# Depthwise taps on TensorE for two images, an offsets' chain with fewer steps, and normalisation over 128 partitions

## The chip, the cores and the metric

The kernel runs on one core of a Trainium2 chip. Its time is the device time of that core in microseconds (us). Five engines work side by side, each through its own instructions in order: TensorE (PE; its weight loads are listed as PEld), VectorE (DVE), ScalarE (ACT), GpSimd (POOL) and SyncE (SP). Transfers are issued by SP, ACT and POOL and run on 16 DMA engines. TensorE's clock is granted in shares of full speed, and the profile shows the share.

## The reference

Two layers over 32 images of 96 channels, 56 x 56, float32. Layer 0 is an inverted bottleneck with squeeze and excitation; layer 1 an attention by spectrum and space, a deformable convolution mixed by a gate with an ordinary one, and a normalisation over the whole batch.

```python
# layer 0
h = silu(bn(conv1x1(x, fake_quant(w1)), g1, b1, m1, v1))            # 96 -> 576
h = silu(bn(depthwise3x3(h, fake_quant(w2)), g2, b2, m2, v2))
s = sigmoid(se_w2 @ silu(se_w1 @ mean(h) + se_b1) + se_b2)
x = x + bn(conv1x1(h * s, fake_quant(w3)), g3, b3, m3, v3)          # 576 -> 96
# layer 1
mag = abs(rfft2(x));  ca = channel_attention(mag);  sa = spatial_attention(x, mag)
y = x * ca * sa
aux = concat([y, coord, freq_e], 1)                                 # 96 + 4 + 1 channels
offset = conv3x3(aux, off_w, off_b)                                 # 18 = 9 taps x 2
gate = sigmoid(conv1x1(relu(conv3x3(aux, dg1_w, dg1_b)), dg2_w, dg2_b))
y_base = conv3x3(y, base_w, base_b)
y_def = einsum(bilinear_samples(y, position + offset), def_w) + def_b
z = (1 - gate) * y_base + gate * y_def
zn = (z - mean(z)) / sqrt(var(z) + 1e-5) * bn_g + bn_b              # over batch and image
return relu(zn + x)
```

## The kernel before, in words

**Layer 0, first part** (`hidden`, with `expand`). An image's 576 hidden channels go in nine units: four chunks of 128 channels by two halves of 28 rows, and one unit that holds both halves of the last 64 channels. `expand` makes a unit's input: a matmul (L163) of seven or eight rows of x (the tile xt, one for each half image, two buffers) and a SiLU on ACT (L167) into one of two padded tiles hp. DVE then does the nine taps of the depthwise convolution on 128 x 1568 elements: a multiply (L224) and eight multiply-adds (L226) into acch. While it does, the next unit is expanded. `finish` applies the second SiLU on ACT (L208), sums for the squeeze, and stores the unit to DRAM (h2d). xt is loaded at the head of `hidden` (L198).

**Layer 0, second part, and the attention** (`attend`). It starts with `squeeze` (L249 to L261), then projects eight row blocks: h2d is loaded again as hq (L274, eight buffers, five for a block), multiplied (L290), the residual is added on POOL (L409) and the sum stored as x1d. Then come two spectral transforms (`dft_mag`) with a chain of small steps between them, whose results are the channel gate ca, the spatial gate sa, and the row fq. The loop multiplies x1d by both into the padded tile yp, eight rows at a time (`refill`), which holds 101 channels: 96 of y, four of coordinates, one of frequency.

**A band** is eight rows of the output, seven to an image, 224 in all. `offsets` makes the sampling weights of one band, two bands ahead. One convolution (`joint_conv`, L548) gives the hidden layer of the gate, the 18 offsets, and 32 of the 96 outputs of the base convolution; a second one (L577) the other 64. DVE adds the offsets' bias (L595) and takes their largest magnitude (L609); POOL adds each position in its 4 x 4 block (L602); the sums go to DRAM (od, L605, issued on POOL) and come back spread over 112 partitions, one copy for each of eight places and fourteen tiles (ht, L614, on SP); ACT makes of them the hat function max(0, 1 - |p - i|) (L617, L618); four transfers issued on POOL (hd, L622) write it to DRAM, from where it is loaded in the layout of the weights for columns and rows (wc and wr, L633 and L634, on SP), and DVE multiplies them (L640). Sampling is then a matmul of blocks of y with these weights (L669), copied out by ACT (L673, L680) and reduced by the deformable convolution (L688). `combine` mixes with the gate, and z goes to DRAM (zd).

**What sets the order.** The parts are generators that give up control at each `yield`. The main loop walks over the bands; at each of the 17 slots of a band it takes a step of `offsets` and, by a due time, steps of two streams: the attention of the next image and the hidden layer of the one after. SP's transfers stay in the order in which the program states them; on the other engines a scheduler may move instructions. Before the main loop, image 0's hidden layer runs alone; then its attention runs, with one step of image 1's hidden layer for each of its steps; then yp is filled, and the offsets of bands 0 and 1 are made.

**The end** (`normalise`). The statistics of z give a scale and a shift for each channel. For each image z and x1d are loaded on 96 partitions (SP and ACT), multiplied and added on DVE (L1220), passed through a Relu on ACT (L1221) and stored (SP, L1222), with three buffers of each. A slower block for offsets that reach further than two pixels stands before it, under a condition; it doesn't run with these inputs.

Of the kernel before, what the change touches and what calls it, by code (L numbers as in the profile page):

```python
# [7 lines left out]
FP = mybir.dt.float32  # L8
# [18 lines left out]
CA = C + 5  # L27
NOFF, NTAP = 18, 9
PD = 2
# [37 lines left out]
HB = HH * W  # L67

# [119 lines left out]
def hidden(tc, p, x, h2d, pooled, defer):  # L188
# [4 lines left out]
    xts = []  # L193

    def rows_of(half):
        xt = p["xt"].tile([C, (HH + 1) * W], FP, name="xt")
        r0 = half * (HH - 1)
        nc.sync.dma_start(xt, x[:, r0 : r0 + HH + 1].rearrange("c h w -> c (h w)"))  # L198
        xts.append(xt)

    rows_of(0)
    rows_of(1)
# [10 lines left out]
    for u, (ch, half) in enumerate(UNITS):  # L213
        h1 = p["h1"]
        more = expand(nc, p, xts, UNITS[u + 1]) if u + 1 < len(UNITS) else iter(())
        acc = p["acch"].tile([128, HH, W], FP, name="acch")
        for n, k in enumerate((4, 0, 1, 2, 3, 5, 6, 7, 8)):
            dy, dx = divmod(k, 3)

            lo, hi = int(half == 0 and dy == 0), HH - int(half == 1 and dy == 2)  # L220
            win = h1[:, dy + lo : dy + hi, dx : dx + W]
            wk = w["w2"][:, ch, k : k + 1]
            if n == 0:
                nc.vector.tensor_scalar(acc, win, wk, None, ALU.mult)  # L224
            else:
                nc.vector.scalar_tensor_tensor(acc[:, lo:hi], win, wk, acc[:, lo:hi], ALU.mult, ALU.add)  # L226
# [163 lines left out]
def attend(tc, p, b, x, h2d, pooled, x1, given=False):  # L390
# [7 lines left out]
    if not given:  # L398
        yield from squeeze(nc, p, pooled)
        rows = [project_loads(nc, p, x, h2d, q) for q in range(2)]  # L400
# [161 lines left out]
def joint_conv(nc, p, yp, j):  # L562
# [4 lines left out]
    conv3(nc, pa[:, :BW], w["joint"], yp, CA, j)  # L567
# [6 lines left out]
    for k in range(NTAP):  # L574
# [3 lines left out]
                         yp[:C, r0 : r0 + RB, dx + PD - 1 : dx + PD - 1 + W], start=(k < 2), stop=(k > NTAP - 3))  # L578
    nc.scalar.activation(yb[:BC], pb[:BC, :BW], AF.Identity, bias=w["cv"]("base_b")[:BC])
# [4 lines left out]
def offsets(nc, p, yp, j, top, hids, ybs, hds):  # L584
# [8 lines left out]
    off = p["off"].tile([NOFF, NTX, 2, TP], FP, name="off")  # L593
    for s in range(2):
        nc.vector.tensor_scalar(off[:, :, s].rearrange("o t (r c) -> o t r c", r=TS),  # L595
                                pa[:, s * BW // 2 : (s + 1) * BW // 2].rearrange("o (r t c) -> o t r c", r=TS, t=NTX),
                                w["offc"], None, ALU.add)
    yield
    yield
    next(joint)  # L600
    at = p["off"].tile([NOFF, NTX, 2, TP], FP, name="at")
    nc.gpsimd.tensor_tensor(at.rearrange("o t s p -> o (t s) p"), off.rearrange("o t s p -> o (t s) p"),  # L602
                            w["place"].unsqueeze(1).to_broadcast([NOFF, 2 * NTX, TP]), ALU.add)
    od = p["dp"].tile([NTX, 2, NOFF, TP], FP, name="od")
    nc.gpsimd.dma_start(od.rearrange("t s o p -> o (t s) p"), at.rearrange("o t s p -> o (t s) p"))  # L605
    yield
    yield
    next(joint, None)
    nc.vector.tensor_reduce(top, off.rearrange("o t s p -> o (t s p)"), AX.X, ALU.max, apply_absolute_value=True)  # L609
    yield  # L610
    yield
    ht = p["ht"].tile([NTX * SB, 4, KP], FP, name="ht")
    src = od.rearrange("t s o p -> t (s o p)").unsqueeze(1).to_broadcast([NTX, SB, 4 * KP])
# [6 lines left out]
    hd = p["dp"].tile([SB, 4, NTX, KP], FP, name="hd")  # L620
    for x in range(4):
        nc.gpsimd.dma_start(hd[:, x].rearrange("i t n -> t i n"), ht[:, x])  # L622
# [3 lines left out]
def weights_load(nc, p, hd, h):  # L626

    src = hd.rearrange("i n t k -> i n (t k)")[:, :, h * NTH * KP : (h + 1) * NTH * KP]
    wc = p["wc"].tile([2 * NS, NTH * KP], FP, name="wc")
    wr = p["wr"].tile([2 * NS, NTH * KP], FP, name="wr")  # L630
    for s in range(2):
        ps = slice(s * NS, (s + 1) * NS)
        nc.sync.dma_start(wc[ps], src[:, 2 * s].unsqueeze(0).to_broadcast([SB, SB, NTH * KP]))  # L633
        nc.sync.dma_start(wr[ps], src[:, 2 * s + 1].unsqueeze(1).to_broadcast([SB, SB, NTH * KP]))  # L634
# [86 lines left out]
def constants(tc, ctx, a, p, gather=False):  # L721
# [34 lines left out]
    load("offc")  # L756
    load("place")
# [91 lines left out]
def padded(nc, p, a, images):  # L849

    cp = p["cp"]
    yps = [cp.tile([CA, HY, WY], FP, name=f"yp{i}") for i in range(images)]
    for t in yps:
        nc.gpsimd.memset(t, 0.0)
        nc.sync.dma_start(t[C : C + 4, PD : PD + H, PD : PD + W], a["coord"])
    p["s4"] = [cp.tile([H, 3, WP], FP, name=f"s4_{i}") for i in range(2)]
# [11 lines left out]
def layers(tc, a, dp, x1d, zd, stats, far):  # L868
# [8 lines left out]
    with ExitStack() as ctx:  # L877
# [12 lines left out]
        def first(b):  # L890
# [5 lines left out]
            return hidden(tc, p, a["x"][b], h2d, pooled, lambda end: later.append((slot + 3, end)))  # L896
# [15 lines left out]
        count = lambda it: sum(1 for _ in it)  # L912
        n_first = count(first(0))
        flush()
        ahead = first(1)
        n_second = 0
        for _ in second(0):
            n_second += 1
            next(ahead, None)
        for _ in ahead:  # L920
            pass
        flush()
# [61 lines left out]
        for r in range(RB, H + 1, RB):  # L984
            refill(0, r)
            flush()
# [6 lines left out]
        for n in range(2):  # L993
            for _ in find(n):
                pass
        n_loads = 0
# [64 lines left out]
        nc.vector.tensor_scalar(far, every, float(REACH), None, ALU.is_gt)  # L1061
# [136 lines left out]
def normalise(tc, a, x1s, zds, stats, out):  # L1198

    nc = tc.nc  # L1200
    with tc.tile_pool(name="nc", bufs=1) as cp, tc.tile_pool(name="np", bufs=3) as tp:
# [12 lines left out]
        inv, sh = bn_affine(nc, cp, col("bn_g"), col("bn_b"), mv[:, 0:1], mv[:, 1:2], "z")  # L1214
        for b in range(B):
            zt = tp.tile([C, HW], FP, name="zt")
            nc.sync.dma_start(zt, zds[b])  # L1217
            xt = tp.tile([C, HW], FP, name="xt")
            nc.scalar.dma_start(xt, x1s[b])  # L1219
# [168 lines left out]
```

## Time and profile before

| | us |
|---|---|
| median of 3 runs | 10260.73 |
| lowest, highest | 10227.61, 10273.77 |
| the profiled execution | 10321.4 |
| its span, from the first to the last instruction | 10319.6 |

How to read the lines that follow below. The busy line of the page gives for each engine busy time, its share of the span, and the instructions. The span is cut in 40 slices with a digit each for busy tenths; PEclk is the granted clock, in tenths. In a table by windows a row is a stretch of time with its length, then busy time and number of instructions of PE, PEld, DVE, ACT and POOL, then the mean granted clock, the mean busy share of the 16 DMA engines, and GB/s moved. A line of waits names who sat idle and at which line, whom it waited for, us in total, how often, and the longest. A group of instructions gives its line, engine, operation, tiles and shape, how often, then total busy us and mean ns.

Durations that the prediction uses, from the groups by shape:

| line, engine, what | mean us |
|---|---|
| L224 DVE, first tap, 128x1568 | 1.03 |
| L226 DVE, further taps, 128x1568 | 1.84 (median of all) |
| L714 DVE, 96x448 with PSUM | 0.679 |
| L715 DVE, 96x448 | 0.936 |
| L602 POOL, positions added, 18x448 | 2.01 |
| L622 POOL, one of four hd issues | 0.574 |
| L1220 DVE and L1221 ACT, 96x3136 | 3.48 and 2.91 |
| L465 ACT, 112x48 | 0.24 |

### The profile page before, as it was taken

To read this page: it belongs to the slowest core of one execution; us is meant where nothing else is said; L and a number is where in the kernel's file an instruction comes from. 1 tells how busy PE (TensorE), PEld (TensorE's weight loads), DVE (VectorE), ACT (ScalarE), POOL (GpSimd) and SP (SyncE) were. 2 spreads that over 40 slices of the span, in tenths; PEclk is the share of its full clock that TensorE was granted. 3 is DMA by queue.
4 is the path that set the end of the run, shared out by engine and by line. 5 is a ranking of instruction groups with operands and counts; after the bars stand their busy time and mean duration, and the time that the engine had idled before them with its cause. 6 is when DMAs were issued, how large, how long until landed. Compare 5 with 4: busy or idle time off the path is not lost. (4 is left out here: it accounts for less than half of the span.)

```text
span 10319.6 us, 123181 instructions
## 1 busy us (share of the span) xinstructions
PE 8859.1 (86%) x43334; PEld 5021.5 (49%) x43334; DVE 7420.8 (72%) x6882; ACT 5342.5 (52%) x10183; POOL 3623.7 (35%) x3759
## 2 busy tenths in 40 slices
PE   2689999999999999999999999999999999999930
PEld 1355555555555555555555555555555555455520
DVE  8677777777777777787777777777777777775322
ACT  1355555555555555555555555555555555554432
POOL 0133433434333344333333333343343343333200
PEclk7789999999999999999999999999999999999865
DMA  1345555554555555455555544555555455555379
GB/s 61 98 135 145 147 146 152 145 137 134 140 144 146 153 150 142 130 143 142 144 142 156 148 137 134 141 144 145 155 148 136 132 140 149 140 150 139 99 210 281
DMA packets 1007994, 1485.64 MB, mean 144 GB/s; under 512 B 619949, under 2 KB 769149, under 8 KB 998154
## 3 DMA queue, kind: packets, MB, share of 16 engines
q1 hardware_dynamic: 873656, 985.19, 36.8%
q0 software_dynamic: 84960, 220.52, 8.5%
q10 hardware_dynamic: 48754, 271.96, 7.2%
q8 instruction: 349, 5.72, 0.3%
q14 instruction: 275, 2.25, 0.1%
HBM read 1064.23 MB, written 412.65 MB: 143 GB/s over the span
## 5 line engine op out<-in xcount | busy, mean ns | idle before, releaser
L226 DVE SCALAR_TENSOR_TENSOR acch<-hp,w,acch 128x1568 f32<-128x1568 f32 (+1 forms) x2304 | 4380.6, 1904 | 33.2
L548 PE MATMUL mm<-yp,c_jointW 101*128 101x448 f32 x4032 | 1688.6, 573 | 11.7 <-DMA yp<-fqd 9.1
L651 POOL COPY ybl<-yp 96x448 f32<-96x448 f32 x896 | 1171.5, 1334 | 1231.0 <-PE mm L655 1230.7
L688 PE MATMUL pd<-v,c_def 128*96 128x224 f32 (+1 forms) x6272 | 1404.2, 373 | 77.1 <-ACT v L680 55.6
L163 PE MATMUL mm<-xt,w 96*128 96x392 f32 (+3 forms) x2688 | 1148.3, 566 | 212.3 <-DMA xt<-in_x 106.5
L669 PE MATMUL mm<-wc,yt 64*96 64x144 f32 x12544 | 1181.4, 302 | 107.8 <-ACT hp L167 57.1
L688 PEld LDWEIGHTS pd<-v,c_def 128*96 128x96 f32 (+1 forms) x6272 | 1033.5, 171 | 366.4 <-ACT v L680 86.4
L548 PEld LDWEIGHTS mm<-yp,c_jointW 101*128 101x128 f32 x4032 | 798.3, 200 | 832.5 <-issue 789.8
L640 DVE TENSOR_TENSOR wc<-wc,wr 128x1008 f32<-128x1008 f32 x448 | 565.8, 1263 | 886.5 <-DMA wr<-hd 771.7
L602 POOL TENSOR_TENSOR at<-off,c_place 18x448 f32<-18x448 f32 x224 | 448.5, 2002 | 1894.6 <-DVE off L595 1894.2
L669 PEld LDWEIGHTS mm<-wc,yt 64*96 64x96 f32 x12544 | 892.4, 163 | 446.4 <-issue 248.6
L290 PE MATMUL mm<-hq,w3s 128*96 128x392 f32 (+1 forms) x2560 | 996.1, 528 | 91.7 <-DMA hq<-h2d 85.0
L673 ACT COPY v<-mm 96x288 f32<-96x288 f32 (+1 forms) x2688 | 999.3, 440 | 100.8 <-PE mm L669 67.6
L167 ACT ACTIVATE hp<-mm,sh,inv 128x392 f32<-128x392 f32 (+2 forms) x1216 | 811.4, 670 | 417.6 <-DVE acch L226 207.5
L208 ACT ACTIVATE acch<-acch,sh,inv 128x1568 f32<-128x1568 f32 x288 | 487.1, 1691 | 987.2 <-DVE acch L226 941.5
L577 PE MATMUL mm<-yp,c_base0W 96*64 96x448 f32 x4032 | 988.9, 590 | 0.0
L622 POOL DMA_DIRECT2D hd<-ht x896 | 509.5, 574 | 785.6 <-ACT ht L618 683.9
L680 ACT COPY v<-v 32x448 f32<-32x448 f32 x1344 | 755.2, 562 | 29.1
L364 PE MATMUL mm<-s,c_GV 112*112 112x464 f32 x1536 | 690.9, 593 | 43.4 <-ACT v L673 36.1
L163 PEld LDWEIGHTS mm<-xt,w 96*128 96x128 f32 (+1 forms) x2688 | 382.8, 189 | 627.9 <-issue 368.4
L290 PEld LDWEIGHTS mm<-hq,w3s 128*96 128x96 f32 (+1 forms) x2560 | 394.4, 169 | 600.0 <-issue 521.3
L577 PEld LDWEIGHTS mm<-yp,c_base0W 96*64 96x64 f32 x4032 | 315.8, 145 | 595.6 <-issue 531.5
(188 smaller groups left out, 9423.3 us busy)
## 6 DMA issues: line engine op xcount, KB each, us to landing
h2d<-acch ACTq DMA_DIRECT2D x288, 784.0 KB
wc<-hd SPq DMA_DIRECT2D x896, 252.0 KB
wr<-hd SPq DMA_DIRECT2D x896, 252.0 KB
hq<-h2d SPq DMA_DIRECT2D x1024, 196.0 KB
x<-x1d SPq DMA_DIRECT2D x768, 98.0 KB
ht<-od SPq DMA_DIRECT2D x224, 252.0 KB
hd<-ht POOLq DMA_DIRECT2D x896, 63.0 KB, 5.4
xt<-in_x SPq DMA_DIRECT2D x64, 609.0 KB
```

Of the source, the lines that this page charges most:

```text
L163: nc.tensor.matmul(pt[p0 : p0 + w1.shape[1], : rows * W], w1, xts[hf][:, r0 * W : (r0 + rows) * W], start=True, stop=True)
L167: nc.scalar.activation(h1[lo:hi, row0 : row0 + rows, 1 : 1 + W], pt[lo:hi, : rows * W].rearrange("p (h w) -> p h w", h=rows), AF.Silu, bia ...
L226: nc.vector.scalar_tensor_tensor(acc[:, lo:hi], win, wk, acc[:, lo:hi], ALU.mult, ALU.add)
L290: nc.tensor.matmul(pt[:C, :EW], w3s[ps, ch], hq[ps], start=(i == 0), stop=(i == NCH - 1))
L364: nc.tensor.matmul(pt[: 2 * W, :n].rearrange("p (q u) -> p q u", q=NPB), w["GV"][:, g], m, start=(k == 0), stop=(k == 1))
L548: nc.tensor.matmul(view, weights[:, k], yp[:channels, r0 : r0 + RB, dx + PD - 1 : dx + PD - 1 + W], start=(k == 0), stop=(k == NTAP - 1))
L577: nc.tensor.matmul(pb[k % 2 * BC : (k % 2 + 1) * BC, :BW].rearrange("p (h w) -> p h w", h=RB), w["base"][:, k], yp[:C, r0 : r0 + RB, dx + ...
L651: nc.gpsimd.tensor_copy(yb[:, :, s], blocks)
L669: nc.tensor.matmul(pt[k][:C, (t - lo) * KP : (t - lo + 1) * KP], yt[ps, t], s[ps, t * KP : (t + 1) * KP], start=True, stop=True)
L673: nc.scalar.copy(v[:C, :, lo:hi, k].rearrange("c k t p -> c t k p"), pt[k][:C, : (hi - lo) * KP].rearrange("c (t k p) -> c t k p", t=hi - ...
L680: nc.scalar.copy(v[C:, 1 + 2 * i : 3 + 2 * i], v[i * QC : (i + 1) * QC, KA:])
L688: nc.tensor.matmul(out.rearrange("c q (t x) -> c t q x", x=TS), p["w"]["def"][ks, k], v[ks, k].rearrange("c t s (r x) -> c t (s r) x", r=T ...
```

## The change

Four parts.

1. **Depthwise taps by TensorE for images 0 and 1.** Three of the nine taps (3, 1 and 5) become matmuls with diagonal weights. `diagonals` builds the fifteen 128 x 128 diagonals on ACT, in the memory of one of the buffers v that the main loop uses later. Per unit twelve matmuls go to four PSUM banks; the first tap on DVE becomes four multiply-adds that read them, and five taps follow. Before the main loop the diagonals are dropped, and later images use nine taps on DVE.
2. **The order around images 0 and 1.** Image 1's hidden layer takes 0.45 steps (`SPREAD`) for each step of image 0's attention, of the filling of yp, and of the first two bands' offsets. In all images the xt halves of the next image are loaded during the hidden layer of the one before, at its units 5 and 8, and the first hq load stands ahead of the squeeze.
3. **The offsets' chain.** Position and bias come out of the joint convolution: yp gets three more channels (column, row, one), so that DVE only copies the offsets out of PSUM, and POOL's addition is gone. ht has the place as its outer index and the tile as its inner one, and one transfer issued on ACT writes hd where four on POOL did. A step is put between the second base convolution and the ACT instruction that copies it out; ht's load comes two steps later. The test for offsets that reach too far looks at place and offset together.
4. **Normalisation over 128 partitions.** Each image is taken as 128 rows of 2352 elements, three pieces of 784, each of one channel. Scale and shift are brought into that layout through DRAM. Loads are all on SP, stores on ACT, with four buffers.

```diff
+def diagonals(nc, p):
+    v = p["vp"].tile([128, NTAP, NTH, 2, TP], FP, name="v")
+    v = v.rearrange("p k t s n -> p (k t s n)")[:, : NCH * len(TPE) * 128].rearrange("p (c k m) -> p c k m", c=NCH, m=128)
+    for ch in range(NCH):
+        for i, k in enumerate(TPE):
+            nc.scalar.mul(v[:, ch, i], p["w"]["ident"], p["w0"]["w2"][:, ch, k : k + 1])
+    return v
...
-    rows_of(0)
-    rows_of(1)
+    xts = p.pop("xts", None) or [rows_of(x, 0), rows_of(x, 1)]
...
+        if xn is not None and u in (5, 8):
+            p.setdefault("xts", []).append(rows_of(xn, int(u == 8)))
...
+        if diag is not None:
+            for r0 in range(0, HH, ER):
+                pt = bank(p)[:, :EW].rearrange("p (h w) -> p h w", h=ER)
+                for i, k in enumerate(TPE):
+                    dy, dx = divmod(k, 3)
+                    lo, hi = rows_of_tap(dy)
+                    lo, hi = max(r0, lo), min(r0 + ER, hi)
+                    nc.tensor.matmul(pt[:, lo - r0 : hi - r0], diag[:, ch, i], h1[:, dy + lo : dy + hi, dx : dx + W],
+                                     start=(i == 0), stop=(i == len(TPE) - 1))
+                parts.append((slice(r0, r0 + ER), pt))
...
+                for rs, pt in parts:
+                    nc.vector.scalar_tensor_tensor(acc[:, rs], win[:, rs], wk, pt, ALU.mult, ALU.add)
+                if not parts:
+                    nc.vector.tensor_scalar(acc, win, wk, None, ALU.mult)
...
+        rows = [project_loads(nc, p, x, h2d, 0)]
         yield from squeeze(nc, p, pooled)
-        rows = [project_loads(nc, p, x, h2d, q) for q in range(2)]
+        rows.append(project_loads(nc, p, x, h2d, 1))
...
-    conv3(nc, pa[:, :BW], w["joint"], yp, CA, j)
+    conv3(nc, pa[:, :BW], w["joint"], yp, CJ, j)
...
+    yield
     nc.scalar.activation(yb[:BC], pb[:BC, :BW], AF.Identity, bias=w["cv"]("base_b")[:BC])
...
-        nc.vector.tensor_scalar(off[:, :, s].rearrange("o t (r c) -> o t r c", r=TS),
-                                pa[:, s * BW // 2 : (s + 1) * BW // 2].rearrange("o (r t c) -> o t r c", r=TS, t=NTX),
-                                w["offc"], None, ALU.add)
-    yield
-    yield
-    next(joint)
-    at = p["off"].tile([NOFF, NTX, 2, TP], FP, name="at")
-    nc.gpsimd.tensor_tensor(at.rearrange("o t s p -> o (t s) p"), off.rearrange("o t s p -> o (t s) p"),
-                            w["place"].unsqueeze(1).to_broadcast([NOFF, 2 * NTX, TP]), ALU.add)
+        nc.vector.tensor_copy(at[:, :, s].rearrange("o t (r c) -> o t r c", r=TS),
+                              pa[:, s * BW // 2 : (s + 1) * BW // 2].rearrange("o (r t c) -> o t r c", r=TS, t=NTX))
+    yield
...
-    hd = p["dp"].tile([SB, 4, NTX, KP], FP, name="hd")
-    for x in range(4):
-        nc.gpsimd.dma_start(hd[:, x].rearrange("i t n -> t i n"), ht[:, x])
+    hd = p["dp"].tile([4, SB, NTX, KP], FP, name="hd")
+    nc.scalar.dma_start(hd.rearrange("x i t n -> (i t) x n"), ht)
...
-            zt = tp.tile([C, HW], FP, name="zt")
-            nc.sync.dma_start(zt, zds[b])
-            xt = tp.tile([C, HW], FP, name="xt")
-            nc.scalar.dma_start(xt, x1s[b])
-            nc.vector.scalar_tensor_tensor(zt, zt, inv, xt, ALU.mult, ALU.add)
-            nc.scalar.activation(zt, zt, AF.Relu, bias=sh)
-            nc.sync.dma_start(out[b].rearrange("c h w -> c (h w)"), zt)
+            zt = tp.tile([128, NQ * QW], FP, name="zt")
+            nc.sync.dma_start(zt, flat(zds[b]))
+            xt = tp.tile([128, NQ * QW], FP, name="xt")
+            nc.sync.dma_start(xt, flat(x1s[b]))
+            for i in range(NQ):
+                part = slice(i * QW, (i + 1) * QW)
+                nc.vector.scalar_tensor_tensor(zt[:, part], zt[:, part], qv[:, 0, i : i + 1], xt[:, part], ALU.mult,
+                                               ALU.add)
+                nc.scalar.activation(zt[:, part], zt[:, part], AF.Relu, bias=qv[:, 1, i : i + 1])
+            nc.scalar.dma_start(flat(out[b].rearrange("c h w -> c (h w)")), zt)
```

## The prediction

> **What bounds the kernel now.** I read the page first, then busy time by stage, then the waits of TensorE and of ScalarE, then short windows around one image's start.
>
> ```profile
> PE 8859.1 (86%) x43334; PEld 5021.5 (49%) x43334; DVE 7420.8 (72%) x6882; ACT 5342.5 (52%) x10183; POOL 3623.7 (35%) x3759
> ...
> PEclk7789999999999999999999999999999999999865
> DMA  1345555554555555455555544555555455555379
> ```
>
> The shares are averages over stages with different limits. Cut at the first depthwise tap (96 us), at the end of image 0's hidden layer (243), at its last attention step (446), at the first sampled tile (492) and at the last band (9901), and with two short windows behind:
>
> ```profile
> 96.00:243.00 147.00, 45.81 (x97) 18.09 (x95) 143.73 (x89) 37.16 (x56) 0.00 (x0) 0.55 0.18 63
> 243.00:446.00 203.00, 116.48 (x382) 63.58 (x383) 159.02 (x122) 69.07 (x117) 30.97 (x35) 0.70 0.31 95
> 446.00:492.00 46.00, 35.72 (x127) 17.39 (x127) 11.66 (x21) 10.08 (x17) 15.67 (x22) 0.83 0.43 105
> 492.00:9901.00 9409.00, 8654.15 (x42717) 4918.41 (x42716) 6937.34 (x6360) 5125.36 (x9951) 3568.12 (x3685) 0.93 0.52 142
> 9901.00:10320.00 419.00, 0.00 (x0) 0.00 (x0) 113.12 (x43) 94.52 (x34) 0.00 (x0) 0.50 0.97 277
> 220.00:240.00 20.00, 0.24 (x2) 0.16 (x2) 19.89 (x13) 4.10 (x6) 0.00 (x0) 0.50 0.10 40
> 9912.00:9936.00 24.00, 0.00 (x0) 0.00 (x0) 4.10 (x2) 2.91 (x1) 0.00 (x0) 0.50 1.01 227
> ```
>
> Columns: PE, PEld, DVE, ACT, POOL busy, granted clock, DMA share, GB/s. 96 to 243 is DVE's (143.7 of 147): nine units of nine taps, with TensorE two thirds idle and at 0.55 of its clock. 492 to 9901 is TensorE's (92%): 224 bands of 42.0 us. 9901 to the end is DMA's (0.97), at 277 GB/s.
>
> TensorE is in order, so each of its 755 idle us in the long stage is on the path. Who ended them, and where ScalarE, which TensorE waits for, was itself held up:
>
> ```profile
> PE mm L290 <- DMA hq<-h2d: 85.0, 35, 4.3
> PE acc L249 <- ACT acch L208: 84.7, 28, 3.6
> ...
> PE mm L163 <- DMA xt<-in_x: 72.9, 29, 6.6
> PE mm L669 <- ACT hp L167: 57.1, 42, 4.4
> PE pd L688 <- ACT v L680: 55.6, 56, 6.1
> ```
> ```profile
> ACT yb L579 <- PE mm L577: 482.8, 214, 6.6
> ...
> ACT ht L617 <- DMA ht<-od: 325.0, 107, 8.1
> ```
> ```profile
> 3736.00:3742.00 6.00, 4.20 (x21) 2.05 (x19) 5.34 (x6) 1.78 (x2) 0.51 (x1) 1.00 1.03 197
> 3742.00:3748.00 6.00, 1.75 (x4) 0.62 (x4) 2.62 (x4) 2.22 (x6) 1.63 (x2) 0.54 0.79 243
> 3748.00:3754.00 6.00, 6.00 (x19) 1.89 (x18) 0.00 (x0) 0.73 (x1) 0.35 (x1) 0.61 0.43 118
> ```
>
> The last fence is the wait for xt at one image's start (4.20 us, after 1.86 us for the squeeze, L249): the granted clock falls to 0.54 and 0.61 for two windows, and comes back. A wait costs its own length and slow matmuls behind it.
>
> **The tail: normalisation.** An image moves 3 x 96 x 3136 x 4 B = 3.61 MB. From the first zt load (9905.9) to the end (10319.6) are 413.7 us, 12.9 an image. DVE and ACT need 3.48 + 2.91 us of it and are hidden. After, they are three pieces of 784 of 3136 columns each: by width 2.6 and 2.2 us, hidden as well. What decides is the rate of transfers over 128 partitions, 9,408 B each. The trace of before has no such load. Bounds: loads of 96 partitions alone run at 227 GB/s with all engines busy (9912 to 9936); the store of 128 partitions (h2d, 0.8 MB) alone moves 40 GB/s at a share of 0.10 (220 to 240), so 400 GB/s at a full share. The new transfers are nearest to the second; I take 385 for loads and stores mixed: 9.4 us an image, 301 for 32. In front comes a new chain: two copies (0.15 us each, as L105), then a DMA to DRAM and one back, each about 2.1 us as sad<-sa, the second issued on SP with all later loads behind it: 5 us. Behind the last load remain DVE, ACT and a store, 9. Sum 315, gain 99; bounds +5 (rate as now) to -111 (400 GB/s: 289 + 14).
>
> [...]
>
> **The first 492 us.** Per unit DVE loses a multiply of 1.03 us (L224) and eight taps of 1.84 (L226), 15.75 us; it gains four 128x392 operations with PSUM and five taps. The nearest row for the first is L714 (96x448 from PSUM, 0.68 us), by width 0.60 (bounds 0.46, at L226's rate, to 0.94, L715's mean): 4 x 0.60 + 5 x 1.84 = 11.6. TensorE gains twelve 392-column matmuls, two records each. Ten records of L290 took 3.62 us at clock 1.00: 0.36 a record, 8.7 us a unit, with expand's four 11.5; at half clock 23. So the two engines come out even, and the clock decides. Since TensorE would be busy almost throughout, as in 256 to 272 where its clock was 1.00, I take the full clock. Unit 0 gains nothing (its taps wait for the first bank, which waits for all of hp), eight units 4.15 each: -33 for image 0. At half clock +60. The 15 diagonals on ACT (15 x 0.3 us; L465, 112x48, took 0.24) lie in its idle time before 89.7, where it waits for the first xt; uncovered 4.5.
>
> Image 1: attention of image 0 has 61 steps, the rows' fill 7, two offset chains 26; at 0.45 that pulls 42 steps, and the layer has 40, so nothing is left over. Six units fall in 243 to 446 and three in 446 to 492. In the first stretch DVE falls from 159 by 9 x 15.75 - 6 x 11.6 = 72 us, but the attention's own hops between engines bind: without the other image its second transform alone took 36 us (410 to 446). In the second stretch TensorE gets 3 x 11.5 on top of 35.7 of 46. I take -23 and +23, so 0; bounds -60 to +30.
>
> **The long stage.** (a) xt of the next image is loaded at units 5 and 8 of the one before, into buffers whose last readers are done: -72.9, and of the clock lost behind it. At 3742 that was 0.46 x 1.75 + 0.39 x 6.00 = 3.1 us; for 29 waits 90, of which I take half, since the squeeze's wait just ahead stays: -45. On SP the two loads stand behind no new wait, about a unit ahead. (b) POOL loses the addition (2.0 us x 224) and three of the four hd issues move away with the fourth to ACT (896 x 0.574). POOL is 38% busy: nothing by itself. But od leaves POOL one step and an addition earlier, while ht's use comes two steps later; with 17 steps a band of 42 us a step is 2.5 us, so the slack of ht grows by some 9 us, over the 8.1 of ACT's longest wait for it. And the extra step ahead of L579 lets ACT do other work while TensorE makes the base convolution. That removes most of 808 us in which ACT stood blocked. TensorE's own waits for ACT (hp, v, yt, sq, without the squeeze) sum to 208 us; bounds 0 to -208, and I take a third, -70, since its stalls also come from ACT's length. (c) ACT gains 224 DMA issues of 0.33 us, 74 us of its 4284 idle. DVE's copies for additions are the same count and size: 0. (d) hq's first load ahead of the squeeze: the wait I looked at (3818) lies at a late row block, held by the eight hq buffers, which stay: 0, bound -85. Sum -188, bounds 0 and -450.
>
> **Sum.** -99 - 33 + 0 - 188 = -320. The profiled execution took 10321.4 (span 10319.6), 0.6% over the median of 10260.73. Made against its own time it is 10001; carried to the median, 9941. I say **9940**.
>
> **Rivals.**
> - Long stage unchanged but for a part of xt: TensorE's stalls for ACT come from the waits for TensorE in a ring (L569 <- L548, 789 us, stays), and the clock still falls behind L249, L383, L499. Then -99 - 33 - 50: 10080. For: the clock is 0.93 on average, and most of the large waits of the list are not touched.
> - The tail's rate is bound behind the partitions, by memory: the share is already 0.97 and a mixed window of 12.9 us averages 280 GB/s. Gain at most 20 there: 10020. Against: 227 and 400 GB/s at full share, by kind.
> - Slower: the hat weights land late. hd now leaves at step 13 instead of 11, 5 us later, less 1.7 for three POOL issues; wc and wr follow it on SP, and DVE already waits 771.7 us for wr in 234 waits, with taps and products queued behind. If TensorE stalls at L669 for it by 1 us in each of 448 halves, +448: 10390. It decides against the gain from 320 / 448 = 0.71 us a half. Against: hd is read half a band (21 us) later, and TensorE waited for wc only once (9.5 us).
> - The diagonals at half clock: DVE waits for TensorE in both images, +60 + 33 and as much in 243 to 492: some 10090.
>
> **Chances.** Forecast, 9830 to 10010: 0.56. Long stage unchanged: 0.18. Tail bound elsewhere: 0.09. Diagonals slow: 0.06. More than forecast (ACT's waits go with their clock): 0.05. Slower: 0.06, a third of which ends within 0.5%. Range 9800 to 10120. A measurement of this kernel can tell 0.5% (51 us) from nothing; by these cases faster 0.93, same 0.03, slower 0.04.
>
> **What would show it.** The stage without TensorE falls from 419 to about 320 at 370 to 400 GB/s. The hidden layer of image 0 takes about 110 us with TensorE's clock near 1; if it stays at 0.55 the step on the clock was wrong. In the long stage the wait for xt is gone, ht's and L579's waits on ACT are under 150 together, and the granted clock is over 0.94; if ACT's waits go and TensorE's stay, (b) was wrong. Waits of DVE for wr beyond 1,500 us, or TensorE waiting for wc, would be the slower case.

## The result and the profile after

| | before | after |
|---|---|---|
| median, us | 10265.58 (10227.61 to 10273.77, 4 runs) | 9930.22 (9912.33 to 9939.44, 4 runs) |
| after / before | | 0.9678 (95% interval 0.9649 to 0.9707) |
| the profiled execution, us | 10321.4 | 9938.4 |
| first depthwise tap at | 95.3 | 85.7 |
| last attention step of image 0 at | 446.1 | 370.5 |
| first sampled tile at (the first stage's length) | 491.7 | 435.8 |
| long stage, to the last band's statistics | 9409 | 9215 |
| from there to the end (from the first zt load) | 419.0 (413.7) | 286.2 (281.0) |

The profiled executions differ by 383.0 us of span: 56 in the first stage, 194 in the long one, 133 in the tail. The medians differ by 335, since the profiled execution of before lies 56 us over its median and that of after 8. The first stage and the tail were the same to a few us in every later kernel that has their code, so most of that scatter is taken to lie in the long stage, whose fall is then about 335 - 56 - 133 = 146 us by the medians.

The page after, with busy time and two of its rows in 40 slices:

```profile
PE 8753.8 (88%) x43766; PEld 5029.2 (51%) x43766; DVE 7220.3 (73%) x6948; ACT 5346.3 (54%) x10262; POOL 2785.4 (28%) x2639
...
PEclk9899999999999999999999999999999999999985
DMA  3345555554555555555555555555545555545549
```

POOL's sum fell most, by 838 us (the addition and the four hd issues had been 958 of it, other operations of POOL took longer than before: the sum with the residual 1.54 us for 1.28, the product of x and sa 2.29 for 2.07), DVE's by 200; TensorE's fell by 105 although 432 matmul records came in. The clock of the first slices rose from 7 and 7 to 9 and 8. By windows, with the columns as before:

```profile
85.50:200.00 114.50, 98.01 (x320) 54.93 (x319) 102.15 (x86) 37.22 (x56) 0.00 (x0) 0.93 0.24 88
200.00:370.50 170.50, 151.67 (x537) 82.05 (x538) 99.96 (x102) 63.38 (x106) 29.13 (x35) 0.91 0.33 98
435.80:9651.00 9215.20, 8441.08 (x42717) 4859.84 (x42717) 6827.24 (x6360) 5125.15 (x9951) 2740.80 (x2576) 0.95 0.54 144
9651.00:9937.00 286.00, 0.00 (x0) 0.00 (x0) 95.57 (x109) 92.32 (x98) 0.00 (x0) 0.50 0.97 405
9670.00:9900.00 230.00, 0.00 (x0) 0.00 (x0) 79.00 (x81) 77.45 (x82) 0.00 (x0) 0.50 1.01 427
```

Image 0's hidden layer (first row) takes 114 us at clock 0.93. In the attention behind it TensorE is busy for 151.7 of 170.5 us. In the long stage the matmul records are the same 42,717 as before, yet TensorE is busy for 213 us less, at a mean clock of 0.95 for 0.93; its idle time stayed (755 before, 774 now). The last row is 230 us of the tail at a steady 427 GB/s.

The waits of TensorE, ScalarE and SyncE after, then SyncE's largest before:

```profile
PE pd L719 <- ACT v L711: 175.1, 36, 8.2
PE mm L323 <- DMA hq<-h2d: 160.5, 66, 7.7
PE pd L719 <- ACT v L704: 138.2, 35, 6.2
PE mm L376 <- POOL x L356: 128.1, 34, 5.0
```
```profile
ACT ht L649 <- DMA ht<-od: 736.3, 186, 9.8
...
ACT yb L614 <- PE mm L611: 442.7, 222, 6.3
```
```profile
SPq L210 <- PE mm L166: 1188.6, 60, 49.5
...
SPq L646 <- DMA od<-at: 901.9, 72, 20.1
```
```profile
SPq L614 <- DMA od<-at: 3029.2, 165, 39.7
```

The waits named in the prediction for xt and the squeeze are gone from TensorE's list of the long stage, and that of L669 for hp fell from 57 to 6 us; waits for the sampled values v (L704, L711: the copies that were L673, L680), for hq and for POOL's x stand there instead, fewer and longer. ACT's wait for ht (now L649) has more than doubled, and that for the base convolution (L614) hardly fell. The xt prefetch (L210) stands 1189 us on SP behind matmuls that still read the old xt.

**How the long stage is counted below.** The trace holds the stretches in which TensorE was granted half its clock. Half of the busy time inside them is counted as work lost to the clock; busy time less that is counted as what the same work takes at full clock. So the stage is work + idle + lost:

```
                 stage   work   idle   lost   idle+lost
before            9409   8096    755    558      1313
after             9215   8071    773    370      1143
```

The work comes out the same within 25 us, as it should if the count is fair. What the clock took fell by 188 us, but idle and lost trade against each other, as two images of before show at one place, the 1.8 us wait at L474 in the attention's chain (16 us from it, by windows):

```profile
5124.00:5140.00 16.00, 15.96 (x71) 10.47 (x72) 8.63 (x8) 8.60 (x22) 3.86 (x7) 0.53 0.77 175
5427.00:5443.00 16.00, 14.44 (x79) 8.85 (x79) 9.06 (x11) 10.08 (x25) 3.85 (x7) 0.89 0.73 169
```

The same wait, at the same place among the same matmuls: once the half clock lasted 20.48 us, once 3.41. The slow image reached the chain's last step (L499) 21.9 us after it without a wait; the quick one stood 3.6 us there and started it after 18.0. The half clock cost 3.9 us net, not the 7.5 that the first row alone suggests (0.47 x 15.96). So kernels are compared by idle + lost, and by their times.

### The profile page after: what moved, and what is told of

Read it like the earlier page. It is cut to its first block, busy times and chain, and to the rows that moved or that the text cites. A ratio compares the mean times of both kernels' runs of the same rounds, so it can differ in the third digit from the quotient of the medians.

```text
span 9936.6 us, 122378 instructions
## 1 busy us (share of the span) xinstructions
PE 8753.8 (88%) x43766; PEld 5029.2 (51%) x43766; DVE 7220.3 (73%) x6948; ACT 5346.3 (54%) x10262; POOL 2785.4 (28%) x2639
## 5 line engine op out<-in xcount | busy, mean ns | idle before, releaser
L259 DVE SCALAR_TENSOR_TENSOR acch<-hp,w,acch 128x1512 f32<-128x1512 f32 (+1 forms) x2250 | 4231.6, 1881 | 34.6
L719 PE MATMUL pd<-v,c_def 128*96 128x224 f32 (+1 forms) x6272 | 1491.5, 391 | 315.0 <-ACT v L711 175.1
L582 PE MATMUL mm<-yp,c_jointW 104*128 104x448 f32 x4032 | 1609.2, 550 | 3.5 <-DMA yp<-fqd 3.5
L582 PEld LDWEIGHTS mm<-yp,c_jointW 104*128 104x128 f32 x4032 | 762.3, 191 | 761.5 <-issue 694.7
L166 PE MATMUL mm<-xt,w 96*128 96x392 f32 (+3 forms) x2688 | 1077.4, 536 | 46.0 <-issue 33.0
L704 ACT COPY v<-mm 96x288 f32<-96x288 f32 (+1 forms) x2688 | 1005.8, 440 | 152.6 <-PE mm L700 120.2
L611 PE MATMUL mm<-yp,c_base0W 96*64 96x448 f32 x4032 | 916.7, 551 | 0.0
L671 DVE TENSOR_TENSOR wc<-wc,wr 128x1008 f32<-128x1008 f32 x448 | 551.9, 1232 | 458.0 <-DMA wr<-hd 349.3
L711 ACT COPY v<-v 32x448 f32<-32x448 f32 x1344 | 755.3, 562 | 28.7
L634 POOL DMA_DIRECT2D od<-at x224 | 185.9, 830 | 2046.4 <-DVE at L630 1655.6
L443 POOL TENSOR_TENSOR o<-o,xc 96x392 f32<-96x392 f32 x256 | 395.1, 1543 | 958.4 <-ACT o L325 955.9
L688 ACT COPY yt<-mm 128x384 f32<-128x384 f32 (+1 forms) x896 | 347.3, 439 | 500.1 <-PE mm L686 484.2
L569 DVE SCALAR_TENSOR_TENSOR yp<-yp,ca,sab 96x448 f32<-96x448 f32 x255 | 157.2, 626 | 576.7 <-DMA yp<-x1d 409.8
```

Source lines behind the costliest of these rows:

```text
L166: nc.tensor.matmul(pt[p0 : p0 + w1.shape[1], : rows * W], w1, xts[hf][:, r0 * W : (r0 + rows) * W], start=True, stop=True)
L582: nc.tensor.matmul(view, weights[:, k], yp[:channels, r0 : r0 + RB, dx + PD - 1 : dx + PD - 1 + W], start=(k == 0), stop=(k == NTAP - 1))
L611: nc.tensor.matmul(pb[k % 2 * BC : (k % 2 + 1) * BC, :BW].rearrange("p (h w) -> p h w", h=RB), w["base"][:, k], yp[:C, r0 : r0 + RB, dx + ...
L704: nc.scalar.copy(v[:C, :, lo:hi, k].rearrange("c k t p -> c t k p"), pt[k][:C, : (hi - lo) * KP].rearrange("c (t k p) -> c t k p", t=hi - ...
L711: nc.scalar.copy(v[C:, 1 + 2 * i : 3 + 2 * i], v[i * QC : (i + 1) * QC, KA:])
L719: nc.tensor.matmul(out.rearrange("c q (t x) -> c t q x", x=TS), p["w"]["def"][ks, k], v[ks, k].rearrange("c t s (r x) -> c t (s r) x", r=T ...
```

## The experiments

Ratios are to before, with their 95% intervals; stages are from one profiled execution each. The intervals are 0.3 to 0.4% wide to either side, so two kernels under some 40 us apart are not told apart by them.

| kernel | median, us | ratio | first sampled tile | long stage | idle + lost | tail |
|---|---|---|---|---|---|---|
| after | 9930.22 | 0.9678 (0.9649 to 0.9707) | 435.8 | 9215 | 1143 | 286.2 |
| tail96 | 9993.33 | 0.9704 (0.9677 to 0.9731) | 436.1 | 9183 | 1112 | 377.9 |
| no_prefetch | 9974.60 | 0.9695 (0.9670 to 0.9721) | 433.9 | 9251 | 1163 | 286.0 |
| chain_only | 10150.45 | 0.9864 (0.9838 to 0.9889) | 477.0 | 9253 | 1162 | 417.8 |
| ht_early | 9975.31 | 0.9691 (0.9666 to 0.9716) | 436.4 | 9300 | 1181 | 286.6 |
| no_step | 9924.42 | 0.9652 (0.9625 to 0.9680) | 436.1 | 9197 | 1127 | 286.2 |
| hd_pool | 9878.28 | 0.9602 (0.9567 to 0.9636) | 435.6 | 9149 | 1073 | 286.5 |
| nine_taps | 9917.77 | 0.9644 (0.9613 to 0.9674) | 429.7 | 9210 | 1138 | 286.1 |
| warm | 10030.66 | 0.9761 (0.9730 to 0.9792) | 436.4 | 9299 | 1128 | 286.1 |
| hd_pool_one | 9865.11 | 0.9622 (0.9586 to 0.9658) | 436.5 | 9132 | 1054 | 286.3 |
| pool_op | 10001.38 | 0.9747 (0.9708 to 0.9785) | 438.4 | 9269 | 1169 | 286.3 |
| nine_pace1 | 9933.59 | 0.9685 (0.9650 to 0.9720) | 477.7 | 9161 | 1092 | 286.6 |
| best | 9828.94 | 0.9574 (0.9539 to 0.9609) | 433.3 | 9114 | 1035 | 286.6 |

**The tail: partitions or queues.** `tail96` keeps the new queues, the four buffers and the pieces of 784 and goes back to 96 partitions.

```diff
-            zt = tp.tile([128, NQ * QW], FP, name="zt")
-            nc.sync.dma_start(zt, flat(zds[b]))
+            zt = tp.tile([C, HW], FP, name="zt")
+            nc.sync.dma_start(zt, zds[b])
...
-            for i in range(NQ):
+            for i in range(4):
...
-            nc.scalar.dma_start(flat(out[b].rearrange("c h w -> c (h w)")), zt)
+            nc.scalar.dma_start(out[b].rearrange("c h w -> c (h w)"), zt)
```

> The changed kernel, but normalisation loads, computes and stores each image on 96 partitions again; queues (loads on SP, stores on ACT), four buffers and pieces of 784 stay. Theory partitions (a transfer over 96 partitions keeps each DMA engine busy longer for the same bytes): the stage without TensorE goes from 286 back to about 410 us, all from the rate (280 to 290 GB/s at full share), and the time is about 10055. Rival queues and buffers (the gain came from taking the stores off SP): the stage stays under 310 and the time is about 9940.

The window of `tail96` behind its first images:

```profile
9720.00:9960.00 240.00, 0.00 (x0) 0.00 (x0) 82.13 (x85) 81.37 (x86) 0.00 (x0) 0.50 1.01 323
```

From the first zt load it takes 372.4 us: 41 less than before, 91 more than after. It lies between what the two theories said. Queues, buffers and the smaller pieces together give the first, the 128 partitions the second. The DMA share is full in all three kernels (0.97 over before's tail, 1.01 in the windows of `tail96` and of after), so the engines do not stand idle less; the same bytes take them less time. Before, SP stood 356 us in front of its stores behind ACT's Relu, with the next zt load queued behind; that wait doesn't exist with stores on ACT. Why a share that was full already then moved more bytes is not shown. With the queues alike, the stage over 128 partitions takes 281.0 / 372.4 = 0.755 of its time over 96, at 427 GB/s for 323.

**The prefetch of xt.** `no_prefetch` loads both halves at the head of the hidden layer again.

```diff
-a["x"][b + 1] if b + 1 < B else None, h2d
+None, h2d
```

> The changed kernel, but xt is loaded at the head of each image's hidden layer, as before. Theory prefetch (the wait for xt and the clock lost behind it were about 118 us of the long stage's gain of 194): the long stage is about 9330 against 9215, with a wait of TensorE for xt of 60 to 80 us, and the time is about 10040. Rival chain (the gain comes from the other places of the offsets' steps among the attention's): long stage 9215 to 9245, time 9930 to 9960.

Waits of TensorE in `no_prefetch`:

```profile
PE mm L166 <- DMA xt<-in_x: 94.8, 29, 7.1
...
PE acc L282 <- ACT acch L219: 58.6, 28, 10.7
```

Both waits are back, 153 us together, and the long stage is 36 us longer; by the ratios it is 17 us slower, inside the intervals. Idle time is the same 774 us with and without them. What TensorE does not wait for at the head of an image, it waits for in another place, as far as these two traces tell.

**The offsets' chain alone.** `chain_only` is the kernel before with part 3 of the change and nothing else.

> The kernel before with the third part alone: place and bias in the joint convolution, one hd transfer on ACT, the step ahead of the base convolution's copy, ht's load two steps later. Theory prefetch: the long stage moves by less than 60 from 9409, time 10200 to 10270. Rival chain: the long stage falls by 120 to 190, the waits for the squeeze (85), for sa (73) and cx (37) are gone, time 10070 to 10150. In both, ACT's wait for ht is over 600 us, if the later load of ht is what made it grow from 325 to 729.

Waits of TensorE and of ScalarE in `chain_only`:

```profile
PE pd L686 <- ACT v L678: 165.0, 35, 7.6
```
```profile
ACT ht L616 <- DMA ht<-od: 648.4, 182, 9.3
```

By the ratio it gains 140 us. 14.7 of them are in the first stage: without the chain's two constants the first tap starts at 83.8 instead of 95.3, since in before the first xt load on SP stood 23.7 us behind the load of one of them, c_place. Some 125 are in the long stage (156 by the profiled executions): most of what the whole change gains there. The new wait for v and the doubled wait for ht come with this part too. The squeeze's wait was to be gone by the rival; 47 of its 85 us in the long stage stayed.

**Which piece of the chain.** `ht_early` issues ht's load two steps earlier, `no_step` takes out the step ahead of the second base convolution's copy, `pool_op` puts an operation of POOL back ahead of od, `hd_pool` and `hd_pool_one` move hd from ACT to POOL, as four transfers and as one.

```diff
 ht_early
-    for _ in range(4):
+    for _ in range(2):
         yield
     ht = p["ht"].tile([SB * NTX, 4, KP], FP, name="ht")
...
-    for _ in range(4):
+    for _ in range(6):
         yield
     nc.scalar.activation(ht, ht, AF.Abs, bias=w["blk"])
 no_step
-    yield
     nc.scalar.activation(yb[:BC], pb[:BC, :BW], AF.Identity, bias=w["cv"]("base_b")[:BC])
 pool_op
+    flat = at.rearrange("o t s p -> o (t s p)")
+    nc.gpsimd.tensor_tensor(flat, flat, w["one"][:NOFF].to_broadcast([NOFF, NTX * 2 * TP]), ALU.mult)
     nc.gpsimd.dma_start(od.rearrange("t s o p -> o (t s) p"), at.rearrange("o t s p -> o (t s) p"))
 hd_pool
-    nc.scalar.dma_start(hd.rearrange("x i t n -> (i t) x n"), ht)
+    for x in range(4):
+        nc.gpsimd.dma_start(hd[x].rearrange("i t n -> (i t) n"), ht[:, x])
 hd_pool_one
-    nc.scalar.dma_start(hd.rearrange("x i t n -> (i t) x n"), ht)
+    nc.gpsimd.dma_start(hd.rearrange("x i t n -> (i t) x n"), ht)
```

> The changed kernel, but ht's load stands two steps earlier in SP's order (four steps behind the copy out of PSUM as before the change), and ACT's use of ht stays where it is. Theory late load (ACT stands 729 us at ht because SP comes to the load 7.7 us after od has landed, and TensorE's 313 us at v are behind that): ACT's wait for ht falls under 250, TensorE's for v under 150, the long stage by 80 to 150 us, time 9790 to 9860. Rival: ACT would wait at another place; SP now stands at ht for od, as before the change (3029 us), hq and wc come later, and the time stays within 9900 to 9980.

ACT's wait for ht and TensorE's largest waits in `ht_early`:

```profile
ACT ht L649 <- DMA ht<-od: 508.6, 176, 7.5
```
```profile
PE acc L288 <- ACT s L285: 113.3, 31, 5.6
...
PE mm L700 <- DVE yb L616: 78.6, 66, 3.1
PE mm L700 <- ACT hp L170: 63.4, 45, 4.4
```

The waits moved as the late load was thought to move them: ht's fell by 228 us, those for v left the top of the list. The time did not follow. Idle fell to 666 us and lost rose to 515. This profiled execution (10024.7) lies 50 us over the median of its kernel, so its long stage of 9300 is too long for the rest of its runs; by the ratios ht_early is 13 us above after, no difference. Where ht's load stands decides which waits there are, and the time does not follow within what the ratios resolve.

> The changed kernel without the step between the second base convolution and the ACT instruction that copies it out. Accounting so far: in each kernel the long stage is TensorE's work at full clock (8070 to 8120 us), plus idle time, plus work lost while the granted clock is one half (558 us before, 370 after). Theory step (the step is what parts TensorE's short waits in the attention's chain): idle stays 700 to 800, the lost work goes back to 450 or more, the long stage is 9290 or more and the time 10000 or more. Rival (ht's later load does it, the step nothing): lost work 350 to 400, long stage 9190 to 9250, time 9910 to 9965.

27 us below after by the ratios, 18 in the long stage: nothing that can be told from no change, and no sign of a gain by the extra step.

> The kernel after with one GpSimd operation put back: ahead of od's issue the 18 x 448 positions are multiplied by one on GpSimd, about 2.0 us in each of 224 bands; the values are unchanged. Theory one, removing the addition mattered (od leaves 2 us earlier in a chain without slack): ScalarE's wait for ht grows from 730 to over 900 us, the long stage by 50 us or more, ratio 0.972 or above. Theory two, the chain has slack and the long stage goes by which short waits meet the clock: ht's wait grows by up to 450 us, but the long stage stays within 30 us of 9215, ratio 0.965 to 0.971.

ScalarE's wait for ht and a wait of VectorE in `pool_op`:

```profile
ACT ht L651 <- DMA ht<-od: 674.4, 164, 8.4
```
```profile
DVE top L643 <- POOL at L635: 187.9, 203, 1.5
```

The operation put back costs 71 us by the ratios and 54 in the long stage: theory one in the time. But ACT's wait for ht did not grow, as both theories had it; it fell by 62 us. Nor is the operation quite the old addition, as the rows of POOL show, of before and of `pool_op`:

```profile
L602 POOL TENSOR_TENSOR at<-off,c_place 18x448 f32<-18x448 f32 x224 | 448.5, 2002 | 1894.6 <-DVE off L595 1894.2
```
```profile
L635 POOL TENSOR_TENSOR at<-at,one 18x448 f32<-18x448 f32 x224 | 379.0, 1692 | 1945.6 <-DVE at L630 1945.3
```

It is 0.3 us shorter, and it writes the tile that DVE's search for the largest offset (L643) reads afterwards. DVE stands behind it there, 188 us in 203 bands. In the kernel before that search read off, which POOL did not write, so this wait is `pool_op`'s own. The 71 us are the price of both together; what the old addition cost alone is not shown.

> The changed kernel, but hd is written by four transfers issued on POOL, as before. Theory of the prediction (POOL's relief is worth nothing by itself): long stage 9185 to 9245, time 9900 to 9965. Rival relief (POOL's waits that TensorE feels, 123 us at the weighed x, come from its queue, and ACT's issue costs nothing): long stage over 9280, time over 9995. If the issue on ACT costs TensorE something at v (313 us), the long stage is below 9170.

> hd is written by one transfer as in the kernel after, but POOL issues it. Theory one, the price of hd in the kernel after is its place on ScalarE: long stage and ratio as with four POOL issues (9149 us, 0.960). Theory two, the price is the single transfer of 252 KB in one queue, which lands later than four of 63 KB: long stage as after (9200 to 9230 us, ratio 0.966 to 0.969), and DVE's wait for the hat weights wr does not fall.

The issue of hd in after, on ACT, and in `hd_pool_one`, on POOL (durations in ns: least, median, most):

```profile
L653 ACTq DMA_DIRECT2D hd<-ht x224: 311/327/1642, 395.3 to 9613.9; - x112
```
```profile
L653 POOL DMA_DIRECT2D hd<-ht x224: 719/737/827, 393.5 to 9532.1; - x112
```

One transfer or four made no difference that can be told (0.9622 and 0.9602); the engine that issues made 57 and 78 us, as theory one of `hd_pool_one` says. The prediction's theory in `hd_pool`, that POOL's relief is worth nothing and the issue on ACT costs nothing, does not hold with its 9149 us.

How the issue's place costs this is not shown. 224 issues of 0.327 us are 73 us of ACT, much the same size, though ACT is idle for 46% of the span, and the longer issue on POOL costs nothing that can be seen. But no line of the waits names the issue, and behind 49 of the 224 in after ACT's next instruction waited for a matmul that ended only after the issue, so those can't have been paid in this way. Nor do the weights come sooner when POOL issues hd; DVE's wait for them, in after and in `hd_pool`:

```profile
DVE wc L671 <- DMA wr<-hd: 349.3, 151, 21.8
```
```profile
DVE wc L672 <- DMA wr<-hd: 445.2, 162, 20.0
```

Idle fell from 773 to 668 and 701 us, lost stayed within 16.

**The start.** `nine_taps` drops the diagonals, `nine_pace1` also the pacing (`SPREAD` 1.0).

```diff
-        p["diag"] = diagonals(nc, p)
...
-SPREAD = 0.45
+SPREAD = 1.0
```

> The changed kernel without the diagonals: images 0 and 1 have nine taps on DVE; pacing by 0.45 and all else stay. Theory taps (DVE decides the first image, TensorE's clock rises with the diagonals): image 0's hidden layer takes 33 to 40 us longer, the first sampled tile comes at 475 to 500 instead of 436, TensorE's clock is near 0.55 in that layer, time 9970 to 9995. Rival pacing (spreading image 1 made the start shorter, the taps little): first sampled tile at 436 to 455, time 9930 to 9950.

> Nine taps on DVE in images 0 and 1, and one step of image 1's hidden layer for each step of image 0's attention, as in the kernel before; the rest as after. With nine taps and 0.45 the main loop began at 429.7 us. Theory one, pacing is what shortened the start: the attention of image 0 ends late again, near 435 us, and the main loop begins at 470 to 480 us as with the offsets' chain alone (477.0); ratio about 0.969. Theory two, the prefetch of xt and hq's earlier load did it, or the kernel is indifferent to the order: the main loop begins at 425 to 440 us, ratio 0.963 to 0.966.

By windows: image 0's hidden layer, its attention, and the rest of the first stage, of `nine_taps` and then of `nine_pace1`:

```profile
84.00:231.00 147.00, 47.00 (x107) 20.43 (x105) 137.62 (x86) 37.10 (x56) 0.00 (x0) 0.56 0.19 68
231.00:382.50 151.50, 105.73 (x362) 56.98 (x363) 133.66 (x103) 63.48 (x106) 37.95 (x35) 0.77 0.38 111
382.50:429.50 47.00, 36.47 (x123) 16.79 (x123) 41.63 (x35) 14.95 (x22) 16.75 (x10) 0.86 0.49 132
```
```profile
83.00:239.00 156.00, 49.27 (x111) 20.96 (x110) 152.24 (x95) 38.90 (x59) 0.00 (x0) 0.54 0.18 64
239.00:434.00 195.00, 113.92 (x377) 61.38 (x378) 151.11 (x115) 68.03 (x115) 31.12 (x36) 0.71 0.34 102
434.00:477.50 43.50, 35.15 (x118) 16.86 (x116) 11.26 (x21) 10.03 (x17) 6.84 (x11) 0.85 0.43 100
```

Without diagonals the hidden layer takes 147 us instead of 114, at half clock, and yet the main loop starts at 429.7, 6 us earlier than with them. The 33 us that the diagonals save are spent behind them: the attention takes 170.5 us with them and 151.5 without, what follows 65.3 and 47.0. With image 1's taps among its matmuls TensorE is busy 151.7 of those 170.5 us; without, 105.7 of 151.5. The pacing is what shortened the start: with 1.0 instead of 0.45 the main loop starts at 477.7, 48 us later. There image 1's layer goes in early (DVE has a unit more in the first row, 95 operations for 86) and makes image 0's attention 195 us long; the last stretch, in which DVE then has little (11 us of 43.5), is only 3.5 us shorter for it. The ratio is 42 us higher, near its resolution.

**Matmuls to keep the clock up.** `warm` puts six matmuls, whose result is not used, ahead of the first matmuls of the second transform, where TensorE waits for POOL's x.

```diff
         yield
+        pw = p["acc"].tile([128, 512], FP, name="acc")
+        for _ in range(6):
+            nc.tensor.matmul(pw[:W, : 3 * 2 * W], gate, w["GV"].rearrange("p g m -> p (g m)"), start=True, stop=True)
     for g in range(NG):
         pt = bank(p)
```

> The changed kernel with six matmuls more (56x336, some 3.4 us at full clock, of the spatial gate, their result is not used) ahead of the second transform of each image, where TensorE waits some 4 us for POOL's weighed x in 30 images (123 us). Theory clock (a wait of this length halves the clock behind it, and 68 us of work are lost there): idle at that place falls from 123 by about 80 to 100, the lost work from 370 to about 300, the long stage by 30 to 80, time 9850 to 9900, though TensorE does 32 x 3.4 = 109 us more work. Rival (the clock falls whatever fills the wait, or falls at another place): lost work 360 or more, long stage 9215 to 9300, time 9930 to 10010.

TensorE's wait in `warm` that after doesn't have:

```profile
PE mm L166 <- ACT s L386: 116.0, 22, 6.0
```

The wait for POOL's x fell from 128 to 5 us and this one came, in the steps behind. Work rose by 100 us (8171), idle + lost fell by 15 only: 85 us lost by the ratios. The added work is in the time almost in full; filling this wait brought nothing forward that can be seen.

**Put together.** `best` is after with hd issued on POOL, without diagonals and without the extra step.

> The kernel after with three parts taken out again: four POOL issues write hd (alone 9878.3, ratio 0.9602), nine taps on DVE for images 0 and 1 (alone 0.9644), and no extra step ahead of the second base convolution's copy (alone 0.9652); after itself stands at 0.9678. If the three gains are of different places they add: ratio 0.9602 - 0.0034 - 0.0026 = 0.954, some 9810 us, with a long stage near 9130 us. If the gains of the last two are measurement scatter and the long stage only shuffles its waits, the ratio stays at 0.958 to 0.962 (9850 to 9890) and the long stage at 9140 to 9170.

0.9574 lies between the two theories' figures, and its interval holds both; the long stage (9114) is on the side of the first. It is faster than after by 101 us by the medians. Of the three parts taken out, hd's issue alone is told apart from nothing when taken out by itself (78 us).

## Why the prediction came out

**The sum came out, and in good part by luck.** 9940 was said and 9930 measured. By parts, said and measured (long stage by the medians; by the profiled executions in brackets): tail -99 and -133; first stage -33 and -56; long stage -188 and -146 (-194). Two parts gained 34 and 23 us more than was said and the third 42 less, so most of it cancels; and within the long stage the two large terms were wrong in opposite ways (118 for xt against 17 to 36, 70 for the chain against 125). The forecast made against the profiled execution, 10001, was 63 us above the 9938 that was profiled.

**The tail.** That transfers over 128 partitions move more was right (427 GB/s for 323 in `tail96`), the term "385 for loads and stores mixed: 9.4 us an image" was mis-sized: 427 GB/s at full share, 8.4 us an image. The bound of 400 was taken from a store at a tenth of the share, and did not hold. By `tail96` the partitions gave 91 us, near the 99 said for all; the other 41, by queues, buffers and pieces, were not in the sum as a gain of their own.

**The first stage.** "-33 for image 0" held where it was placed: 147 us became 114, at clock 0.93, near the full clock assumed. It was the wrong place to count: the next step, image 1's "-23 and +23, so 0", took as even a trade in which the attention got longer once image 1's taps were among its matmuls. `nine_taps` shows no gain by the diagonals in all, `nine_pace1` the pacing worth 48 us, which the prediction had at 0 (bounds -60 to +30), and `chain_only` some 12 us by the two dropped constants, which it left out.

**The long stage: the size came out, the reasons did not.**
- (a) "-72.9, and of the clock lost behind it", for which another 45 was taken: the wait went and the gain did not follow, 17 to 36 us instead of 118. The step that failed is the one from "each of its 755 idle us in the long stage is on the path" to a gain of a wait's length when it is taken away: idle was 774 us with this wait and without it. "On SP the two loads stand behind no new wait" was wrong as well: 1189 us.
- (b) "That removes most of 808 us in which ACT stood blocked": over the whole trace those two waits went from 823 to 1179 us. ht's load, too, leaves two steps later, and its use stands four steps behind it as before, so the slack counted on did not come between these two; why the wait doubled is not shown. The yb copy's wait fell by some 40 us, but `no_step`, without the step, has the same 440 us and the same time. TensorE's own waits for ACT, which (b) was to cut from 208 us by 70, rose to 366, while those for DVE fell from 218 to 101. The gain of the chain, 125 us in `chain_only`, is thus not the one that (b) described.
- (b) also had "POOL is 38% busy: nothing by itself". `pool_op` puts an operation in the addition's place at 71 us, together with a wait of DVE that the addition did not cause; so this is in doubt, and not refuted.
- (c) "74 us of its 4284 idle", counted as nothing, was wrong: 57 and 78 us in two kernels. The idle share of ACT was taken for cover.
- (d), hq's first load, was not tried by itself.
So the chain gains 125 us in the long stage although its hd issue costs 57 to 78, and for what it gains before that cost the only piece found is the addition, with the 71 us of `pool_op` in doubt. Where the rest comes from stays open. ht's place and the extra step are each within 40 us of nothing. od's earlier step, the copies on DVE and the new layout of ht and hd were not tried alone.

**The rivals.** "Long stage unchanged" was right that the list of waits would fill again, and wrong on the time: idle did stay, the clock's losses fell. That the weights land late was wrong: DVE's wait for wr fell from 771.7 to 349.3 us, while SP's wait in front of ht's load fell from 3029 to 902. With ht early again (`ht_early`) these were 755.3 and 2510, at a time within 13 us of after: that wait bore nothing either way. A rate bound by memory, with 20 us of gain at most, was wrong at 427 GB/s. The diagonals did run near full clock.

## What to carry to other kernels

An idle share is no proof of cover: an issue of 0.33 us a band on ScalarE, 46% idle, cost 57 to 78 us; ask what is queued behind it, and try it on another engine. Removing a wait of the busiest engine need not pay: here 153 us of waits went and the same idle time stood in other places; compare idle plus what the clock took, not the list of waits. Cut a change into its parts before keeping it: here one part lost in one place what it gained in another, and leaving three pieces out was faster by 101 us. A test that puts a piece back may bring a wait of its own, as `pool_op` did; look for new lines in its waits before reading its price.

## What the hardware showed that was not expected

- The half clock came in multiples of 3.41 us (in before 188 of 189 stretches, 183 of them of 3.41 to 20.48; the last one, through the tail, ends with the profile), and one wait of 1.8 us was followed by 3.41 in one image and 20.48 in another. In the image with 20.48 TensorE was busy 15.96 of 16 us by the profile, which models the ends of matmuls, and still had a mean clock of 0.53, with small matmuls of the attention among those of a band.
- Loads and stores over 128 partitions ran at 427 GB/s for 230 us, evenly, on one core; over 96 partitions at 323 for 240 us, with the same queues and the same full share of the DMA engines.
- Seven runs of the kernel before, on one chip, went from 10235.84 us at a mean clock of 0.909 to 10308.59 at 0.901, the lowest of the seven: the same program's scatter goes roughly with the clock.
